# Three-pass gates in eighteen more steps, a plain first product, and an order shifted by a list of moves

## The chip, the cores and the metric

The kernel runs on one core of one Trainium2 chip. The metric is the device time of one execution in microseconds; the number compared is the median of several runs. Beside it stands one profiled execution, whose trace gives the span from the first to the last instruction and the duration of each instruction. The engines are named as in the profile: PE (TensorE, matmuls), PEld (its weight loads, which overlap), DVE (VectorE), ACT (ScalarE), POOL (GpSimd), and SP, whose queue issues nearly all DMAs.

## The reference, cut to what matters

A batch of 32 graphs shares one adjacency matrix of 512 x 512; each node has 128 features. Four layers follow each other, each with a layer norm and a ReLU in front and a residual around it.

```
h = relu(layernorm(x));  x = x + (A_norm @ h) @ W.T + b          # layer 0
h = relu(layernorm(x));  x = x + ggnn(h)                          # layer 1
h = relu(layernorm(x));  x = x + elu(attention(h, adj))           # layer 2
h = relu(layernorm(x));  x = x + attention(h, adj)                # layer 3

def ggnn(h):                       # 5 steps; both matrices are adj
    m  = adj @ h ;  av = [m, m]
    z  = sigmoid(av @ w3.T + h @ u3.T + biases)
    r  = sigmoid(av @ w4.T + h @ u3.T + biases)
    hv = tanh(av @ w5.T + (r * h) @ u5.T + biases)
    h  = (1 - z) * h + z * hv
```

All data are fp32. Since av is m twice, each gate needs one product of m with the sum of two halves of a weight.

## The kernel before, in words

**Tiles.** One batch is one tile of 128 partitions x 512 elements (four chunks of 128 nodes), one PSUM bank wide. PSUM is cut into eight such banks. A batch lives in SBUF through all four layers.

**Stages.** `gcn` is layer 0 for a pair of batches, `ggnn` is layer 1 with five calls of `step`, and `gat` is an attention layer, called twice per batch. For batches 0 to 3 the first layer uses plain products (`product`, L658), from batch 4 on `in_three`. Up to six batches (lanes) are in `ggnn` at a time, while others are in `gcn` and `gat`.

**Products in three passes.** A plain fp32 matmul leaves two records in the trace. `in_three` (L628) replaces it: `operands` (L614) splits the moving tile into upper (ACT, L617), lower (DVE, L618) and across (DVE, L620), and the matrix has been split once into three factors by `factors_of` (L418). Each term is then a matmul in the one-pass format fp32r. Two passes are summed in the bank, ACT rescales the bank in place (`rescale`, L625), and the third pass is added. So a product of adj and h is 12 one-pass matmuls (L644) and one rescaling.

**Gates.** `step` (L750) computes the three gates. `by_m` (L760) multiplies m by a gate weight, either plainly (L755, where m has been copied from PSUM by ACT, L655) or in three passes (L758). For three passes m itself is split by `operands` (L654), each gate's bank is rescaled between its second and third pass, and a fourth rescaling by the inverse stands between the gates r and z, which share a bank (L793). The products of hT by u3 and of r * h by u5 stay plain (L755). `SPLIT_GATES` (L29) says which steps take three passes: all five of batches 2 to 29. Batches 0, 1, 30 and 31 take their gates plainly.

**The order.** Nothing is written in program order. Every operation is given to a planner (`Plan`, L60) with its engine, a cost, a due time, and what it reads and writes. The planner plays the program through as a list schedule (`attempt`, L167): on each engine the ready operation with the smallest `soon` starts, if its buffers are free. `run` (L105) makes eight trials for each of two settings; in the later trials an operation's `soon` is its latest start in a pass backwards (`put_off`, L138), and only operations that started at or before `near_end` (0 us) keep their written due time. The best trial's order is emitted. The loads at the start, the factors and the norms are operations like any other; each engine and SP's queue then run their list in that order.

**The norm.** `norm_relu` (L516) makes mean and variance on DVE, four small operations on POOL (L520 to L525), which the planner takes to cost 1.2 us each, and four scaled ReLUs on ACT (L527).

**The end.** Attention of the last four batches (`near`) avoids round trips through DRAM; the largest piece of DVE work there is L914 (four per attention), PE mixes in L926.

Of the kernel before, what the change touches and what calls it, by code (L numbers as in the profile page):

```python
# [10 lines left out]
F32 = mybir.dt.float32  # L11
# [3 lines left out]
ALU = mybir.AluOpType  # L15

P = 128
EPS = 1e-5
STEPS = 5
# [6 lines left out]
IDLE_FROM = 1342  # L26
RUN_UP = 8
LANES = 6
SPLIT_GATES = {(b, s) for b in range(2, 30) for s in range(STEPS)}  # L29

# [5 lines left out]
SPLIT = 4096.0  # L38
BELOW = 1 - 2.0 ** -13
# [20 lines left out]
class Plan:  # L60
# [44 lines left out]
    def run(self):  # L105


        self.before = {o: [] for o in self.ops}
        for o in reversed(self.ops):
            o.tail = o.cost + o.delay + max((q.tail for q in o.then), default=0)  # L110
            o.first, o.after = o.waits, len(o.then)
            for q in o.then:
                self.before[q].append(o)
        self.uses = {v: v.uses for o in self.ops for v in o.vals}
        best = math.inf, None
        for last, hurry in self.ends:
            for again in range(8):
                if again:
                    late = self.put_off()
                for o in self.ops:  # L120
                    if not again:

                        o.soon = min(o.due, last - o.tail * hurry)
                    else:
                        o.soon = late[o] / self.SLOT if o.at > self.near_end else o.due
                self.attempt()
                if self.end < best[0]:
                    best = self.end, [o.soon for o in self.ops]
                if self.end == math.inf:
                    break  # L130
        assert best[1], "the order has come to a stop"
        for o, soon in zip(self.ops, best[1]):
            o.soon = soon
        self.attempt()
        for o in self.order:
            o.emit()

    def put_off(self):  # L138

# [131 lines left out]
def gnn_stack(ctx: ExitStack, tc: tile.TileContext, a: dict, out: bass.AP):  # L271
    nc = tc.nc
    x, adj = a["x"], a["adj"]
    B, N, D = x.shape
    C = N // P
# [9 lines left out]
    def flat(t):  # L285
# [31 lines left out]
        "rstd": tiles(8, SMALL, "rstd"),  # L317
        "off": tiles(6, SMALL, "off"),
        "rden": tiles(3, SMALL, "rden"),
    }, [(167, 0.1), (181, 0.05)], 0,  # L320
        IDLE_FROM, lambda v: nc.tensor.transpose(v.t[:, 0, :], ident.t, ident.t))
    op = plan.op
    MM, MM1, TURN, MR = 0.858, 0.224, 0.111, 0.2325
# [71 lines left out]
    turned = []  # L395
# [22 lines left out]
    def factors_of(mT, name, due, *then):  # L418


        upper, lower, across = [fixed([P, C, N], name + k, C, dtype=F32R) for k in ("1", "2", "3")]
        for c in range(C):
            op("ACT", COPY, due, lambda c=c: nc.scalar.mul(upper.t[:, c, :], mT.t[:, c, :], BELOW), r=[mT, *then], w=[upper[c]])
            op("DVE", V, due, lambda c=c: nc.vector.tensor_sub(
                lower.t[:, c, :], mT.t[:, c, :], upper.t[:, c, :].bitcast(F32)), r=[mT, upper[c]], w=[lower[c]])
            op("DVE", V, due, lambda c=c: nc.vector.scalar_tensor_tensor(
                across.t[:, c, :], upper.t[:, c, :].bitcast(F32), -1 / SPLIT, lower.t[:, c, :].bitcast(F32),
                op0=ALU.mult, op1=ALU.add), r=[lower[c], upper[c]], w=[across[c]])
            op("ACT", COPY, due, lambda c=c: nc.scalar.mul(
                lower.t[:, c, :], lower.t[:, c, :].bitcast(F32), SPLIT), w=[lower[c]])  # L430
        return upper, lower, across

    def edges(l, c, mask, at, due, *then):
# [38 lines left out]
    def factors_of_gates(due):  # L472
        upper, lower, across = [fixed([P, 3, P], "gates" + k, dtype=F32R) for k in ("1", "2", "3")]
        some = gates.t[:, 1:, :]
        op("ACT", 0.4, due, lambda: nc.scalar.mul(upper.t, some, BELOW), r=[gates], w=[upper])
        op("DVE", 0.47, due, lambda: nc.vector.tensor_sub(lower.t, some, upper.t.bitcast(F32)), r=[gates, upper], w=[lower])
        op("DVE", 0.47, due, lambda: nc.vector.scalar_tensor_tensor(
            across.t, upper.t.bitcast(F32), -1 / SPLIT, lower.t.bitcast(F32), op0=ALU.mult, op1=ALU.add),
           r=[lower, upper], w=[across])
        op("ACT", 0.4, due, lambda: nc.scalar.mul(lower.t, lower.t.bitcast(F32), SPLIT), w=[lower])  # L480
        return upper, lower, across
    of_gates = factors_of_gates(5)
    u5T = transposed(-15.2, (one(raw["u5"]), 0.5), then=turned)
# [32 lines left out]
    def norm_relu(b, y, due, times=None):  # L516

        xb, off, rstd = xs[b], Val("off"), Val("rstd")
        mv = norm_stats(b, due)
        op("POOL", 1.2, due, lambda: nc.gpsimd.tensor_tensor(rstd.t, mv.t[:, :, 1], eps.t, ALU.add), r=[mv, eps], w=[rstd])  # L520
        op("POOL", 1.2, due, lambda: nc.gpsimd.tensor_tensor(rstd.t, rstd.t, mhalf.t, ALU.pow), r=[mhalf], w=[rstd])  # L521
        op("POOL", 1.2, due, lambda: nc.gpsimd.tensor_tensor(off.t, mv.t[:, :, 0], minus1.t, ALU.mult), r=[mv, minus1], w=[off])
        if times:
            op("DVE", 0.1, due, lambda: nc.vector.tensor_mul(rstd.t, rstd.t, times.t), r=[times], w=[rstd])
        op("POOL", 1.2, due, lambda: nc.gpsimd.tensor_tensor(off.t, off.t, rstd.t, ALU.mult), r=[rstd], w=[off])  # L525
        for c in range(C):
            op("ACT", 0.385, due, lambda c=c: nc.scalar.activation(  # L527
                chunk(y, c), xb.t[:, c, :], AF.Relu, bias=off.t[:, c:c + 1], scale=rstd.t[:, c:c + 1]),
               r=[xb[c], off, rstd], w=[y[c * len(y.writers) // C]])
# [27 lines left out]
    def center_relu(b, y, due):  # L557

        xb, st, mv, off, ve, rstd = xs[b], Val("st", C), Val("mv", 2), Val("off", 2), Val("ve"), Val("rstd")
        for a in range(2):  # L560
            both = slice(2 * a, 2 * a + 2)
            for c in (2 * a, 2 * a + 1):
                op("DVE", 0.2, due, lambda c=c: nc.vector.bn_stats(st.t[:, c, :], xb.t[:, c, :]), r=[xb[c]], w=[st[c]])  # L563

            def aggr(a=a, both=both):
                for c in (2 * a, 2 * a + 1):
                    nc.vector.bn_aggr(mv.t[:, c, :], st.t[:, c, :])
                nc.vector.tensor_scalar_mul(off.t[:, both], mv.t[:, both, 0], -1.0)
            op("DVE", 0.22, due, aggr, r=[st[2 * a], st[2 * a + 1]], w=[mv[a], off[a]])
            for c in (2 * a, 2 * a + 1):  # L570
                op("ACT", 0.385, due, lambda c=c: nc.scalar.activation(
                    y.t[:, c, :], xb.t[:, c, :], AF.Relu, bias=off.t[:, c:c + 1]), r=[xb[c], off[a]], w=[y[c]])
        op("DVE", 0.1, due, lambda: nc.vector.tensor_scalar_add(ve.t, mv.t[:, :, 1], EPS), r=[mv], w=[ve])
        op("POOL", 1.0, due, lambda: nc.gpsimd.tensor_tensor(rstd.t, ve.t, mhalf.t, ALU.pow), r=[ve, mhalf], w=[rstd])
        return rstd

    def chunk(h, c):
# [44 lines left out]
           r=[lower, upper], w=[across])  # L622
        return upper, lower, across

    def rescale(p, due, by=1 + 1 / SPLIT):  # L625
        op("ACT", COPY, due, lambda: nc.scalar.mul(flat(p.t), flat(p.t), by), w=[p])  # L626

    def in_three(h, turned, factors, due, split=False):  # L628
# [26 lines left out]
        op("ACT", COPY, due - 6, lambda: nc.scalar.copy(flat(m.t), flat(p.t)), r=[p], w=[m])  # L655
        return m

    def product(h, due):  # L658

        p, m = Val("bank"), Val("m")  # L660
        for c in range(C):
            def times(c=c):
                row = adjT.t[:, c, :]
                terms = [(0, c, row[:, :c * P]), (c, c + 1, diag.t[:, c, :]), (c + 1, C, row[:, (c + 1) * P:])]
                for lo, hi, right in terms:
                    if lo < hi:
                        nc.tensor.matmul(flat(p.t)[:, lo * P:hi * P], h.t[:, c, :], right, start=c == lo == 0,  # L667
                                         stop=c == C - 1, skip_group_check=True)
            op("PE", MM, due, times, r=[h[c], adjT, diag[c]], w=[p, m])
        op("ACT", COPY, due, lambda: nc.scalar.copy(flat(m.t), flat(p.t)), r=[p], w=[m])  # L670
        return m

# [23 lines left out]
    def gcn(pair, due):  # L696
# [8 lines left out]
                xs[b].t, xs[b].t, b0.t[:, None, :].to_broadcast([P, C, D])), r=[b0], w=[xs[b]])  # L705
            ys.append(y)

        ms = [product(y, due + i) if first else in_three(y, False, factors["an"], due + i) for i, y in enumerate(ys)]
        if b == 1:
            factors["adj"] = factors_of(adjT, "adj", -3.6, ys[0])  # L710
            factors["an"] = normalized(ms[0])
# [19 lines left out]
    def ggnn(b, due):  # L731
# [9 lines left out]
        turned = False  # L741
        for s in range(STEPS):
            now = due + LANES * s
            split = (b, s) in SPLIT_GATES
            m = in_three(h, turned, factors["adj"], now, split)
            if b == 4 and s == 0:
                op("SP", 0.0, now, lambda: None, r=[m[0] if split else m], w=[third], delay=0)
            h, turned, hT = step(b, s, m, hT, now, lane)

    def step(b, s, m, hT, due, lane):  # L750
# [39 lines left out]
        op("DVE", V, due - 5, lambda: nc.vector.scalar_tensor_tensor(flat(rh.t), flat(r.t), 1.0, flat(hT.t), op0=ALU.add, op1=ALU.mult),  # L790
           r=[r, hT], w=[rh])
        if split:
            rescale(gate, due - 5, 1 / (1 + 1 / SPLIT))  # L793
        by_m(gate, 2, due + 0.3, False)
        op("ACT", A, due - 5, lambda: nc.scalar.activation(flat(z.t), flat(gate.t), AF.Tanh, bias=gate_b["w3"].t, scale=0.5),  # L795
           r=[gate, gate_b["w3"]], w=[z])
# [238 lines left out]
```

## Time and profile before

| what | value |
|---|---|
| median of three runs | 1515.34 us (1513.87 to 1516.15) |
| the profiled execution's own time | 1513.58 us |
| its span, first to last instruction | 1511.7 us |
| PE busy | 1498.9 us, 99% |
| DVE busy | 1430.9 us, 95% |
| ACT busy | 1236.2 us, 82% |
| POOL busy | 292.9 us, 19% |
| granted TensorE clock | 1.000 |
| share of the DMA engines' time, main queue | 39.6% |

Times are microseconds from the start of the span unless marked ns. A group line names the source line, the engine, the operation, output<-input, the shapes and the count; then the busy time and the mean duration of one in ns; then the idle time of the engine ahead of these instructions and who ended it. In the slices, each digit is the busy share of one fortieth of the span in tenths. A piece of the chain has its start, its length, and the line with the number of instructions in it. DVE and ACT records overlap a little when instructions follow each other closely, so their spacing is shorter than a record.

### The profile page before, as it was taken

Reading aid. Unit: us, or ns where it says so; the run is one execution under the profiler, and the core shown is the slowest. Engines: PE = TensorE matmul, PEld = TensorE weight load, DVE = VectorE, ACT = ScalarE, POOL = GpSimd, SP = SyncE. Lnnn points to the kernel's source line nnn. Section 1 sums busy time; section 2 is a strip of 40 time slices with the busy share of each in tenths; the row PEclk is TensorE's granted clock in tenths of the full one; section 3 lists DMA queues with packets and bytes.
Section 4 is the critical chain, followed back from the end, with each engine's and each line's share of the span. In section 5 each row is a group of like instructions: output and inputs, shape, how many; then the busy total and the mean of one; then the engine's idle time right before and its main releaser. Section 6 shows DMA issues by size and latency. Waiting matters only on the chain.

```text
span 1511.7 us, 24916 instructions
## 1 busy us (share of the span) xinstructions
PE 1498.9 (99%) x7366; PEld 1153.8 (76%) x7366; DVE 1430.9 (95%) x3431; ACT 1236.2 (82%) x2720; POOL 292.9 (19%) x496
## 2 busy tenths in 40 slices
PE   8999999999999999999999999999999999999998
PEld 7666677777777777777787877877777787767788
DVE  8989989999999999999999999999999999898798
ACT  7966888888888888988889888798988978877764
POOL 5412010221221211220222121111221110111111
PEclk9999999999999999999999999999999999999999
DMA  4143333444434444444444453444434444342111
GB/s 112 36 95 108 84 90 106 116 122 119 112 102 116 126 120 127 124 112 105 124 120 101 113 133 105 113 119 120 126 91 127 120 104 118 86 132 71 36 41 44
DMA packets 270151, 157.77 MB, mean 104 GB/s; under 512 B 81248, under 2 KB 236224, under 8 KB 270016
## 3 DMA queue, kind: packets, MB, share of 16 engines
q1 hardware_dynamic: 269728, 155.66, 39.6%
q8 instruction: 58, 0.95, 0.3%
q14 instruction: 77, 0.63, 0.1%
q10 hardware_dynamic: 288, 0.52, 0.1%
HBM read 86.25 MB, written 69.84 MB: 103 GB/s over the span
## 4 chain that ended last, share of the span: by engine, by line
PE 95%; DVE 3%; ACT 1%; DMA 1%; issue 0%; ACTq 0%
PE bank L644 34%; PE bank L755 21%; PE bank L758 19%; PE bank L940 13%; PE bank L871 4%; PE bank L717 2%; PE bank L926 1%; PE bank L586 1%; DVE e L914 1%; DMA rh<-in_L_gnn_w_w_dram 0%; DMA e<-in_adj_dram 0%; PE bank L667 0%; DVE x L721 0%; DVE st L563 0%; DVE e L685 0%
## 5 line engine op out<-in xcount | busy, mean ns | idle before, releaser
L626 ACT ACTIVATE bank<-bank 128x512 f32<-128x512 f32 x748 | 426.6, 595 | 103.3 <-PE bank L644 72.8
L520 POOL TENSOR_TENSOR rstd<-mv,eps 128x4 f32<-128x4 f32 x119 | 59.2, 497 | 1110.2 <-DVE mv L512 1049.1
L940 PEld LDWEIGHTS bank<-h_gat,e 128*128 128x128 f32 x1792 | 218.1, 191 | 24.2 <-issue 17.0
L620 DVE SCALAR_TENSOR_TENSOR across<-lower,upper 128x512 fp32r<-128x512 f32 x328 | 219.7, 676 | 4.2 <-PE bank L758 2.4
L940 PE MATMUL bank<-h_gat,e 128*128 128x129 f32 x1792 | 220.3, 275 | 0.0
L758 PE MATMUL bank<-upper,gates 128*128 128x512 f32 x420 | 205.2, 489 | 0.0
L758 PE MATMUL bank<-across,gates 128*128 128x512 f32 x420 | 198.8, 487 | 0.2 <-ACT bank L626 0.2
L644 PE MATMUL bank<-adj,upper 128*128 128x512 f32 x640 | 189.6, 418 | 0.7 <-ACT upper L617 0.7
L644 PE MATMUL bank<-adj,across 128*128 128x512 f32 x640 | 189.8, 419 | 0.0
L644 PE MATMUL bank<-adj,lower 128*128 128x512 f32 x640 | 175.4, 396 | 0.0
L758 PE MATMUL bank<-lower,gates 128*128 128x512 f32 x420 | 165.5, 394 | 0.0
L755 PE MATMUL bank<-hT,wT 128*128 128x512 f32 x320 | 163.3, 592 | 0.0
L755 PE MATMUL bank<-rh,wT 128*128 128x512 f32 x320 | 163.3, 592 | 0.0
L914 DVE SCALAR_TENSOR_TENSOR e<-row,h_gat,maskT 128x512 f32<-128x512 f32 x224 | 156.8, 741 | 0.0
L644 PEld LDWEIGHTS bank<-adj,across 128*128 128x128 f32 x640 | 118.3, 188 | 42.4 <-issue 16.5
L644 PEld LDWEIGHTS bank<-adj,upper 128*128 128x128 f32 x640 | 118.3, 188 | 41.1 <-issue 14.4
L644 PEld LDWEIGHTS bank<-adj,lower 128*128 128x128 f32 x640 | 120.5, 188 | 28.6 <-DVE lower L618 0.4
L788 ACT ACTIVATE r<-bank,gate_bw 128x512 f32<-128x512 f32 x160 | 111.7, 698 | 36.8 <-PE bank L755 34.6
L521 POOL TENSOR_TENSOR rstd<-rstd,mhalf 128x4 f32<-128x4 f32 x119 | 135.6, 1140 | 0.0
L801 DVE TENSOR_TENSOR hv<-hv,hT 128x512 f32<-128x512 f32 x160 | 108.7, 680 | 19.1 <-ACT hv L799 18.3
L795 ACT ACTIVATE z<-bank,gate_bw 128x512 f32<-128x512 f32 x160 | 110.4, 692 | 18.1 <-PE bank L758 15.4
L799 ACT ACTIVATE hv<-bank,gate_bw 128x512 f32<-128x512 f32 x160 | 111.2, 696 | 11.9 <-PE bank L755 11.7
(162 smaller groups left out, 2843.3 us busy)
## 6 DMA issues: line engine op xcount, KB each, us to landing
far<-sq SPq DMA_DIRECT2D x928, 64.0 KB
h<-far SPq DMA_DIRECT2D x148, 256.0 KB
gT<-far SPq DMA_DIRECT2D x56, 256.0 KB
row<-line SPq DMA_DIRECT2D x56, 256.0 KB
hT<-far SPq DMA_DIRECT2D x112, 64.0 KB
x<-in_x_dram SPq DMA_DIRECT2D x24, 256.0 KB
out_dram<-x SPq DMA_DIRECT2D x20, 256.0 KB
adjT<-in_x_dram SPq DMA_DIRECT2D x8, 256.0 KB
```

The source lines that it names most:

```text
L521: op("POOL", 1.2, due, lambda: nc.gpsimd.tensor_tensor(rstd.t, rstd.t, mhalf.t, ALU.pow), r=[mhalf], w=[rstd])
L620: op("DVE", V, due - 5, lambda: nc.vector.scalar_tensor_tensor(flat(across.t), flat(lower.t).bitcast(F32), -SPLIT, flat(upper.t).bitcast(F ...
L626: op("ACT", COPY, due, lambda: nc.scalar.mul(flat(p.t), flat(p.t), by), w=[p])
L644: nc.tensor.matmul(flat(p.t), left.t[:, c, :], right.t[:, c, :], start=first and c == 0, stop=c == C - 1, skip_group_check=True)
L755: nc.tensor.matmul(flat(p.t), (of or gates).t[:, i, :], flat(moving.t), start=start, stop=True, skip_group_check=True)
L758: nc.tensor.matmul(flat(p.t), of.t[:, i - 1, :], flat(moving.t), start=start, stop=True, skip_group_check=True)
L788: op("ACT", A, due - 5, lambda: nc.scalar.activation(flat(r.t), flat(gate.t), AF.Tanh, bias=gate_b["w4"].t, scale=0.5), r=[gate, gate_b["w ...
L795: op("ACT", A, due - 5, lambda: nc.scalar.activation(flat(z.t), flat(gate.t), AF.Tanh, bias=gate_b["w3"].t, scale=0.5), r=[gate, gate_b["w ...
L799: op("ACT", A, due - 5, lambda: nc.scalar.activation(flat(hv.t), flat(cand.t), AF.Tanh, bias=gate_b["w5"].t), r=[cand, z, gate_b["w5"]], w ...
L801: op("DVE", V, due - 5, lambda: nc.vector.tensor_sub(flat(hv.t), flat(hv.t), flat(hT.t)), r=[hT], w=[hv])
L914: op("DVE", 0.661, due + 3, lambda j=j: nc.vector.scalar_tensor_tensor(e.t[:, j, :], matrix(row), h.t[:, j, D + 1:D + 2], mask.t[:, j, :], ...
L940: nc.tensor.matmul(pt()[:, c, :D + 1], e.t[:, j, i * P:(i + 1) * P], h.t[:, j, :D + 1], start=(j == 0), stop=(j == C - 1))
```

## The change

1. Three-pass gates in all steps but two. `SPLIT_GATES` gives way to `WHOLE_GATES`, the steps that stay plain: the first steps of batches 0 and 1.
2. The first step of batch 0 (`WHOLE`) takes its adjacency product in plain fp32 by `product`, which gets a flag `loops`; with the flag off the rows of adjT are used whole.
3. The scale of the split of the fixed matrices: the upper factor is divided by SPLIT = 4096, the lower factor is made with its scale at once, so its separate scaling on ACT is dropped. The bank is rescaled by SPLIT + 1 instead of 1 + 1 / SPLIT, and by the inverse between r and z.
4. The planner: other POOL costs, `near_end` 12 instead of 0, ten trials instead of eight, and `nudge`. For each number of a list it draws a window of time, a share and a distance from a hash, and shifts `soon` of that share of the operations that started in the window, if they started after `near_end`, by a hashed amount up to that distance, forwards or backwards.

```diff
-SPLIT_GATES = {(b, s) for b in range(2, 30) for s in range(STEPS)}
+WHOLE = {(0, 0)}
+WHOLE_GATES = {(0, 0), (1, 0)}
+
+NUDGES = (
+    582105, 147139, 36044, 562756, 451743, 52419, 574539, 43563, 131, 944493, 237051, 489767, 324034, 993924,
...
+)
...
-            for again in range(8):
+            for again in range(10):
...
-        for o, soon in zip(self.ops, best[1]):
-            o.soon = soon
+        self.nudge(*best)
         self.attempt()
...
+    def nudge(self, end, soon, at):
...
+        for o, t in zip(self.ops, soon):
+            o.soon = t
+        for n in NUDGES:
+            a, b, c, d = (mixed(n * 2654435761 + j * 40503) / 2.0 ** 32 for j in range(1, 5))
+            width = 20 * 40 ** a
+            begin, share, far = b * (end + width) - width, 65536 * 0.01 ** c, 0.02 * 100 ** d
+            for o, t in zip(self.ops, at):
+                if max(self.near_end, begin) < t < begin + width:
+                    m = mixed(n * 2654435761 + o.id * 2246822519 + 77)
+                    if (m & 0xffff) < share:
+                        o.soon += far * ((m >> 16) / 32768 - 1)
...
-    }, [(167, 0.1), (181, 0.05)], 0,
+    }, [(167, 0.1), (181, 0.05)], 12,
...
-            op("ACT", COPY, due, lambda c=c: nc.scalar.mul(upper.t[:, c, :], mT.t[:, c, :], BELOW), r=[mT, *then], w=[upper[c]])
+            op("ACT", COPY, due, lambda c=c: nc.scalar.mul(upper.t[:, c, :], mT.t[:, c, :], BELOW / SPLIT), r=[mT, *then], w=[upper[c]])
+            op("DVE", V, due, lambda c=c: nc.vector.scalar_tensor_tensor(
+                lower.t[:, c, :], upper.t[:, c, :].bitcast(F32), -SPLIT, mT.t[:, c, :], op0=ALU.mult, op1=ALU.add),
+               r=[mT, upper[c]], w=[lower[c]])
             op("DVE", V, due, lambda c=c: nc.vector.tensor_sub(
-                lower.t[:, c, :], mT.t[:, c, :], upper.t[:, c, :].bitcast(F32)), r=[mT, upper[c]], w=[lower[c]])
-            op("DVE", V, due, lambda c=c: nc.vector.scalar_tensor_tensor(
-                across.t[:, c, :], upper.t[:, c, :].bitcast(F32), -1 / SPLIT, lower.t[:, c, :].bitcast(F32),
-                op0=ALU.mult, op1=ALU.add), r=[lower[c], upper[c]], w=[across[c]])
-            op("ACT", COPY, due, lambda c=c: nc.scalar.mul(
-                lower.t[:, c, :], lower.t[:, c, :].bitcast(F32), SPLIT), w=[lower[c]])
+                across.t[:, c, :], lower.t[:, c, :].bitcast(F32), upper.t[:, c, :].bitcast(F32)),
+               r=[lower[c], upper[c]], w=[across[c]])
...
-        op("POOL", 1.2, due, lambda: nc.gpsimd.tensor_tensor(rstd.t, mv.t[:, :, 1], eps.t, ALU.add), r=[mv, eps], w=[rstd])
-        op("POOL", 1.2, due, lambda: nc.gpsimd.tensor_tensor(rstd.t, rstd.t, mhalf.t, ALU.pow), r=[mhalf], w=[rstd])
-        op("POOL", 1.2, due, lambda: nc.gpsimd.tensor_tensor(off.t, mv.t[:, :, 0], minus1.t, ALU.mult), r=[mv, minus1], w=[off])
+        op("POOL", 0.5, due, lambda: nc.gpsimd.tensor_tensor(rstd.t, mv.t[:, :, 1], eps.t, ALU.add), r=[mv, eps], w=[rstd])
+        op("POOL", 1.15, due, lambda: nc.gpsimd.tensor_tensor(rstd.t, rstd.t, mhalf.t, ALU.pow), r=[mhalf], w=[rstd])
+        op("POOL", 0.42, due, lambda: nc.gpsimd.tensor_tensor(off.t, mv.t[:, :, 0], minus1.t, ALU.mult), r=[mv, minus1], w=[off])
...
-    def rescale(p, due, by=1 + 1 / SPLIT):
+    def rescale(p, due, by=SPLIT + 1):
...
-    def product(h, due):
+    def product(h, due, loops):
...
-                terms = [(0, c, row[:, :c * P]), (c, c + 1, diag.t[:, c, :]), (c + 1, C, row[:, (c + 1) * P:])]
+                terms = [(0, C, row)]
+                if loops:
+                    terms = [(0, c, row[:, :c * P]), (c, c + 1, diag.t[:, c, :]), (c + 1, C, row[:, (c + 1) * P:])]
...
-            split = (b, s) in SPLIT_GATES
-            m = in_three(h, turned, factors["adj"], now, split)
+            split = (b, s) not in WHOLE_GATES
+            m = product(h, now, False) if (b, s) in WHOLE else in_three(h, turned, factors["adj"], now, split)
...
-            rescale(gate, due - 5, 1 / (1 + 1 / SPLIT))
+            rescale(gate, due - 5, 1 / (SPLIT + 1))
```

`factors_of_gates` (L472) is changed in the same way as `factors_of`, with one operation of 384 elements in place of four of 512. The list has 175 numbers.

## The prediction, made before the changed kernel was built

> **What bounds the kernel now.** I read the busy table and the forty slices first, then the chain of work that ended last, then a table of busy times by stage, then the groups of instructions by shape, and last the timeline of the tail.
>
> ```profile
> PE 1498.9 (99%) x7366; PEld 1153.8 (76%) x7366; DVE 1430.9 (95%) x3431; ACT 1236.2 (82%) x2720; POOL 292.9 (19%) x496
> ...
> PE   8999999999999999999999999999999999999998
> ...
> DVE  8989989999999999999999999999999999898798
> ACT  7966888888888888988889888798988978877764
> ...
> PE 95%; DVE 3%; ACT 1%; DMA 1%; issue 0%; ACTq 0%
> ```
>
> TensorE (PE) is full in all but the first and last slices, and 95% of the chain lies on it. VectorE (DVE) is close behind. So what leaves PE shortens the kernel, provided that DVE keeps up. The chain also gives PE's true prices, because its pieces run from start to start:
>
> ```profile
> 45.31 2.79 PE bank L644 x12
> ...
> 51.20 2.57 PE bank L755 x6
> ...
> 644.79 2.10 PE bank L758 x9
> ```
>
> Twelve one-pass matmuls of an adjacency product take 2.79 us. Three plain products with 512 columns (each two records) take 2.57 us, 0.857 each. Nine one-pass gate matmuls take 2.10, so a gate product in three passes costs 0.70. By stage (columns: stage, PE, weight loads, DVE, ACT, POOL, clock, DMA):
>
> ```profile
> 60.00:100.00 40.00, 40.00 (x153) 27.41 (x152) 34.73 (x77) 31.97 (x65) 7.48 (x12) 1.00 0.37 82
> 100.00:150.00 50.00, 50.00 (x188) 33.95 (x187) 45.87 (x124) 32.27 (x58) 11.28 (x24) 1.00 0.38 102
> 150.00:200.00 50.00, 50.00 (x190) 34.40 (x189) 45.81 (x89) 43.38 (x87) 4.61 (x8) 1.00 0.33 80
> ...
> 1300.00:1340.00 40.00, 40.00 (x179) 28.73 (x178) 36.85 (x77) 32.60 (x73) 4.18 (x8) 1.00 0.37 103
> 1340.00:1380.00 40.00, 40.00 (x177) 28.27 (x176) 34.38 (x79) 29.40 (x60) 4.89 (x11) 1.00 0.38 104
> 1380.00:1420.00 40.00, 40.00 (x203) 29.85 (x202) 34.68 (x76) 32.77 (x77) 6.54 (x7) 1.00 0.21 55
> 1420.00:1460.00 40.00, 40.00 (x235) 30.88 (x235) 33.48 (x101) 24.83 (x65) 5.78 (x7) 1.00 0.13 40
> 1460.00:1512.00 52.00, 45.94 (x404) 45.03 (x402) 46.91 (x160) 24.11 (x85) 4.06 (x5) 0.98 0.14 42
> ```
>
> The reader should see PE at 40 of 40 up to 1460 us, DVE with some idle time in the same stages, and a tail after 1460 in which neither is full. PE's idle time in the whole span is 1511.7 - 1498.9 = 12.8 us: 5.8 before 60 us, 1.3 in the middle, about 6 in the tail. In the tail PE waits for DVE:
>
> ```profile
> 1496.43 1.16 PE L926 MATMUL bank<-h_gat,e 128*128 128x129 f32 x8 [1.08 <-DVE e L914]
> ...
> 1501.42 6.42 PE L926 MATMUL bank<-h_gat,e 128*128 128x129 f32 x56
> ```
>
> **What the Trainium skill says.** FP8 and Floating Point Precision, TensorE Precision Notes: true fp32 takes four passes through the array, the reduced form reads fp32 and truncates. The trace agrees: 0.857 us against 0.233, 3.7 to one, so three single passes undercut one true fp32 product. VectorE: DVE Perf Modes, the section on the TRN2 errata, prices a vector operation from SBUF at 58 + FD cycles of 0.96 GHz, 594 ns for 512 elements; in this trace full-width DVE operations follow each other at 0.60 us (records of 0.68 overlap). Perfetto Trace Analysis, Optimization Strategy: a kernel can have regimes with different most-contended engines, and the gaps of each regime must be read by themselves. That holds here: PE up to 1460 us, DVE from then on.
>
> **The change, part by part.** Eighteen more steps take the gates in three passes: steps 1 to 4 of batches 0 and 1, and all ten of batches 30 and 31. Their plain m products lie at 37 to 193 us and at 1284 to 1459 us (120 records, twenty steps).
>
> - PE, removed: 18 steps x (2.57 - 2.10) = 8.5 us, 3.8 early and 4.7 late, all on the chain except perhaps the last step or two, which end where the tail begins.
> - PE, added: the first step of batch 0 takes its adjacency product in plain fp32, 4 x 0.857 = 3.43 instead of 2.79, +0.6. It no longer waits for the factors of adj, at a time (before 40 us) when PE has gaps and DVE is full, so this may cost nothing; I count it in full. Net PE: -7.8 us.
> - DVE, added: a split step makes the lower and across operands of m:
>
> ```profile
> L618 DVE TENSOR_TENSOR lower<-bank,upper 128x512 fp32r<-128x512 f32 x140 | 94.7, 676 | 9.7 <-ACT upper L617 9.2
> L626 ACT ACTIVATE bank<-bank 128x512 f32<-128x512 f32 x748 | 426.6, 595 | 103.3 <-PE bank L644 72.8 <-PE bank L758 28.2
> L429 ACT ACTIVATE adj<-adj 128x512 fp32r<-128x512 f32 x4 | 2.5, 632 | 0.7 <-DVE adj L426 0.7
> ```
>
>   18 x 2 x 0.60 = 21.6 us, less 1.2 for batch 0's first step. Early that is 8 x 1.2 = 9.6 us, where DVE has 13.6 us idle between 60 and 200 us (140 - 126.4); PE's saving takes 3.8 of that, so DVE would stand at 99%. Some of its work can slide into the stages after 200 us. Late it is 12 us, where DVE has 20.6 us idle between 1300 and 1460 and loses 4.7 to the shorter PE stage. So the work fits with little to spare in both places. If that cover is gone, each missing microsecond of DVE costs one.
> - ACT, added: four rescalings of a bank and one upper in place of the copy of m, so 4 x 0.595 = 2.4 us a step, 43 us in all, less 5.5 us for nine removed scalings of the factors (four of 632 ns, four of 621, one of 517) and some 1.2 for the first step. ACT is idle 32.4 us of the 140 early (19 needed) and 40.4 of the 160 late (24 needed). It is not the bound, but an ACT instruction now stands between the second and third pass of each gate, and r, z and hv queue behind it on ACT. A step becomes some 3 to 4 us longer; in the middle of the kernel, where 140 such steps already run, PE's waits for such rescalings sum to 14.2 us of weight loads in 48 places and are hidden behind other matmuls. PE costs nothing from this while other lanes have work, but the last step of batch 31 (its m product at 1458 us) feeds the tail directly.
> - For these waits and the full DVE I take +1.0 early (bounds 0 and 3.8, all of the saving) and +1.2 late (bounds 0 and 4.7): the late value is the two new DVE operations of the very last step.
> - The factors keep their number of DVE operations, with subtract and multiply-add exchanged (676 to 686 ns each); the rescaling by 4097 is the same instruction with another constant. Zero.
> - Order: the planner's POOL costs fall from 1.2 to what the trace shows (0.50, 1.14, 0.39, 0.44 us), operations that started before 12 us keep their written order, ten trials replace eight, and the list shifts due times. No instruction is added. The written order issues the gate weights w4 and w3 on SP's queue before the loads of x for batches 1 to 3; before, w4 was issued at 5.55 us and PE waited for it until 10.37. What is moved is the loads of x1 to x3, by a microsecond or two, with their statistics on DVE behind them. PE's first product also waits for the normalised batch 0, so at most 1 us is gained here, and about as much can be lost.
> - What a better order can reach at all: 12.8 us of PE idle, less 1.05 before the first matmul and 3.9 after the last one, leaves 7.9. The bounds are -7.9 and, if a shuffled order leaves new holes on the chip, +3. I take half of the 7.9: -4.0.
>
> Sum: -7.8 + 1.0 + 1.2 - 4.0 = -9.6 us. On the profiled execution: span 1511.7 - 9.6 = 1502.1, its own time 1513.58 - 9.6 = 1504.0. The median of the three runs shown is 1.76 above that execution: 1515.34 - 9.6 = 1505.7.
>
> **The rivals.**
> - Nearly all reachable holes close and DVE hides everything: -7.8 - 7.9 = -15.7, so 1499.6. For it: a long list of moves can serve many holes. Against: the tail is DVE work that waits for the last batches, and more DVE work is added.
> - The tail swallows the late part: DVE ends when it ended before, so the 4.7 late are lost and the order gives nothing. Then -3.8 + 0.6 + 1.0 = -2.2, so 1513.1. For it: from 1432 us on DVE has hardly a hole of more than half a microsecond. Against: the 20.6 us of idle time just ahead.
> - Slower: DVE becomes the bound of the late stage. Its holes before 1460 us are waits for results of the last lanes (2.3 us for hv at 1426), and if only u of the needed 12 us falls into them, the end moves by 12 - u, with the early part still at -2.2: faster than before only while u is over 9.8, and out of measurement's reach on the slow side below u = 6.8. With u = 4 it gives -2.2 + 8 = +5.8, so 1521.1. Against it: the middle of the kernel runs with DVE at 99.5% (500 to 700 us, 199.0 of 200) and PE full.
> - The list moves nothing that matters (order 0): -5.6, so 1509.7; it belongs to the forecast's own range.
>
> **How the numbers follow.** A measurement of this kernel can tell about 0.2%, 3.0 us, from no change: 1512.3 to 1518.4 is "same". Forecast 0.58 (own range 1501.5 to 1511), all holes closed 0.14, tail swallows 0.17, slower 0.11. Of the third, a third falls below 1512.3, the rest within; of the fourth, 0.03 stays within. Faster 0.58 + 0.14 + 0.06 = 0.78, same 0.11 + 0.03 = 0.14, slower 0.08. The range 1498 to 1515 leaves out about 0.05 below and 0.12 above.
>
> **What would show it.** In the profile after: plain gate products of m in 12 records instead of 120; gate groups of 474 in place of 420; rescalings 819 in place of 748; PE busy some 8 us less (1491); DVE busy 1451; no scaling of lower in the factors. PE still full from some 40 us to beyond 1440 would show that DVE hid the new work; PE idle in the first 200 us or from 1300 on with DVE as releaser would show that it did not. PE idle of about 9 us in all would confirm the order's term. The prediction is wrong if DVE's idle time before 1460 us stays as large as it was while the tail begins later, or if PE's price for a three-pass gate at the two ends is above 0.70.

## The result, and the profile after

| what | before | after |
|---|---|---|
| median of five runs | 1515.34 us (1513.65 to 1516.15) | 1510.13 us (1508.32 to 1513.26) |
| ratio | | 0.9969, 95% interval 0.9955 to 0.9982 |
| profiled execution: own time, span | 1513.58, 1511.7 us | 1510.13, 1508.2 us |

The change is faster by 0.31%, 4.7 us with an interval of 2.7 to 6.8; forecast were 9.6. (The ratio is made from all runs of both kernels; the two medians alone are 5.2 us apart.) Measured again on another occasion it gave 1510.37 us, ratio 0.9974 (0.9964 to 0.9983). Its runs lie 5 us apart, those of before 2.5.

The page of the profile after: the busy table, the slices of PE, DVE and ACT, and the chain that ended last.

```profile
PE 1494.0 (99%) x7416; PEld 1160.5 (77%) x7416; DVE 1446.5 (96%) x3465; ACT 1258.1 (83%) x2781; POOL 294.6 (20%) x496
...
PE   9999999999999999999999999999999999999998
...
DVE  8999989999999999999999999999989999998999
ACT  6788888888988898878888888888878798978874
...
DVE 5%; PE 1%; issue 0%; ACT 0%; POOL 0%; DVEq 0%
```

The counts are as the prediction had them (PE 7366 - 54 x 2 + 162 - 12 + 8 = 7416). But PE is busy only 4.9 us less, and its idle time, 1508.2 - 1494.0 = 14.2 us, has grown from 12.8 although the span is shorter. The chain is no help here: its shares add up to some 6% because it could be followed back only through the tail. The stages say where PE stands still (columns as in the prediction's table):

```profile
40.00:60.00 20.00, 17.28 (x72) 12.54 (x71) 16.69 (x53) 14.60 (x31) 8.38 (x17) 1.00 0.14 27
...
100.00:150.00 50.00, 50.00 (x198) 35.88 (x197) 49.83 (x126) 41.22 (x78) 12.39 (x22) 1.00 0.40 103
...
500.00:700.00 200.00, 198.80 (x995) 155.78 (x994) 195.05 (x456) 168.02 (x372) 40.00 (x66) 1.00 0.44 115
700.00:900.00 200.00, 198.49 (x972) 153.25 (x971) 194.00 (x447) 168.59 (x375) 39.47 (x67) 1.00 0.44 114
...
1420.00:1460.00 40.00, 39.78 (x252) 33.19 (x251) 39.11 (x105) 33.44 (x89) 6.13 (x8) 1.00 0.17 47
1460.00:1512.00 52.00, 44.28 (x381) 42.71 (x379) 45.23 (x164) 24.38 (x82) 5.47 (x5) 0.97 0.14 41
```

The kernel before, in two of these stages:

```profile
500.00:700.00 200.00, 200.00 (x998) 156.26 (x997) 199.01 (x459) 172.92 (x389) 36.82 (x64) 1.00 0.46 121
700.00:900.00 200.00, 200.00 (x988) 156.44 (x987) 194.79 (x474) 169.75 (x371) 44.82 (x76) 1.00 0.45 116
```

Between 100 and 150 us DVE is full (49.8 of 50) and PE loses nothing; from 1300 to 1460 us PE loses 0.5 us in all. So the added work at the two ends is nearly hidden. The holes are elsewhere: one of 2.7 us in 40 to 60 us, and new ones in the middle of the kernel, where no step was changed. Before, PE was full from 60 to 1100 us. From 60 to 1300 us PE's idle time grew from 1.3 to 4.4 us. The waits name the new waiter: ScalarE's ReLUs of the norm, which wait for the last GpSimd operation of that norm (total, times, longest). Before:

```profile
ACT y L527 <- POOL off L525: 0.4, 1, 0.4
```

After, 24.6 us in all:

```profile
ACT y L565 <- POOL off L563: 19.2, 15, 3.8
ACT h L565 <- POOL off L563: 5.4, 3, 3.4
```

The timeline around one such hole shows the whole way (start, length, engine, line; in brackets the idle time and who ended it):

```profile
604.84 0.67 DVE L841 TENSOR_TENSOR hv<-hv,hT 128x512 f32<-128x512 f32 x1
605.42 0.69 DVE L658 SCALAR_TENSOR_TENSOR across<-lower,upper 128x512 fp32r<-128x512 f32 x1
605.48 3.10 POOL L558 TENSOR_TENSOR rstd<-mv,eps 128x4 f32<-128x4 f32 x1
...
607.83 0.69 DVE L658 SCALAR_TENSOR_TENSOR across<-lower,upper 128x512 fp32r<-128x512 f32 x1
608.43 0.71 DVE L632 STREAM_TRANSPOSE sq<-hT 128x512 f32<-128x512 f32 x1
608.53 0.20 POOL L563 TENSOR_TENSOR off<-off,rstd 128x4 f32<-128x4 f32 x1
...
608.76 1.65 ACT L565 ACTIVATE y<-x,off,rstd 128x128 f32<-128x128 f32 x4 [3.80 <-POOL off L563]
...
610.32 0.57 ACT L664 ACTIVATE bank<-bank 128x512 f32<-128x512 f32 x1
...
610.94 1.20 PE L682 MATMUL bank<-adj,across 128*128 128x512 f32 x4 [1.01 <-ACT bank L664]
```

A GpSimd addition of 4 elements per partition, which takes 0.2 us when it is short, takes 3.10. It ends with the run of VectorE operations with two SBUF tensors (604.84 to 608.52), as the first VectorE operation with one input, a transpose, begins. The addition belongs to the next norm, but it stands in GpSimd's queue ahead of the multiplication (608.53) that the ReLUs need. ScalarE has put four ReLUs next in its queue and waits 3.80 us; behind them stands the rescaling of a bank; PE needs that bank and stops. The holes at 44 us (2.7), 847 us (1.5) and 1114 us (1.4) begin in the same way, behind GpSimd operations of 5.1, 3.0 and 2.1 us. What stands behind the ReLUs differs: at 44 us a copy of m for PE, at 847 us a rescaling, at 1114 us an operand that VectorE needs before PE.

### The profile page after: what moved, and what is told of

Read it like the earlier page. It is cut to its first block, busy times and chain, and to the rows that moved or that the text cites. A ratio compares the mean times of both kernels' runs of the same rounds, so it can differ in the third digit from the quotient of the medians.

```text
span 1508.2 us, 25120 instructions
## 1 busy us (share of the span) xinstructions
PE 1494.0 (99%) x7416; PEld 1160.5 (77%) x7416; DVE 1446.5 (96%) x3465; ACT 1258.1 (83%) x2781; POOL 294.6 (20%) x496
## 5 line engine op out<-in xcount | busy, mean ns | idle before, releaser
L664 ACT ACTIVATE bank<-bank 128x512 f32<-128x512 f32 x819 | 464.9, 595 | 85.2 <-PE bank L682 59.2
L798 PE MATMUL bank<-upper,gates 128*128 128x512 f32 x474 | 232.9, 491 | 0.4 <-ACT bank L664 0.2
L658 DVE SCALAR_TENSOR_TENSOR across<-lower,upper 128x512 fp32r<-128x512 f32 x345 | 230.6, 677 | 2.7 <-PE bank L798 0.9
L558 POOL TENSOR_TENSOR rstd<-mv,eps 128x4 f32<-128x4 f32 x119 | 54.3, 456 | 894.9 <-DVE mv L550 842.7
L798 PE MATMUL bank<-across,gates 128*128 128x512 f32 x474 | 217.7, 473 | 0.0
L798 PE MATMUL bank<-lower,gates 128*128 128x512 f32 x474 | 186.7, 394 | 0.0
L559 POOL TENSOR_TENSOR rstd<-rstd,mhalf 128x4 f32<-128x4 f32 x119 | 143.5, 1206 | 1.3
L565 ACT ACTIVATE y<-x,off,rstd 128x128 f32<-128x128 f32 x252 | 113.0, 497 | 15.4 <-POOL off L563 15.1
L798 PEld LDWEIGHTS bank<-across,gates 128*128 128x128 f32 x474 | 88.8, 188 | 45.2 <-ACT bank L664 19.9
```

The lines of the kernel that those rows point to most:

```text
L558: op("POOL", 0.5, due, lambda: nc.gpsimd.tensor_tensor(rstd.t, mv.t[:, :, 1], eps.t, ALU.add), r=[mv, eps], w=[rstd])
L559: op("POOL", 1.15, due, lambda: nc.gpsimd.tensor_tensor(rstd.t, rstd.t, mhalf.t, ALU.pow), r=[mhalf], w=[rstd])
L565: op("ACT", 0.385, due, lambda c=c: nc.scalar.activation(chunk(y, c), xb.t[:, c, :], AF.Relu, bias=off.t[:, c:c + 1], scale=rstd.t[:, c:c ...
L798: nc.tensor.matmul(flat(p.t), of.t[:, i - 1, :], flat(moving.t), start=start, stop=True, skip_group_check=True)
```

## Theories and experiments

**Theory A.** GpSimd's small operations are locked out while VectorE runs operations with two SBUF inputs. The order now leaves them no slack, because the plan takes them at their mean duration, and ScalarE's queue carries the delay to PE. **Theory B.** An order pressed by a list of moves is fragile by itself; any jitter opens holes. **Theory C.** The added VectorE work of the eighteen steps fills VectorE, and that costs what is missing.

All times are medians, with the ratio to the kernel before in runs of the same occasion and its 95% interval.

### GpSimd's part left out, in the order of after and of before

```diff
-        op("POOL", 0.5, due, lambda: nc.gpsimd.tensor_tensor(rstd.t, mv.t[:, :, 1], eps.t, ALU.add), r=[mv, eps], w=[rstd])
+        small(0.5, due, lambda: nc.gpsimd.tensor_tensor(rstd.t, mv.t[:, :, 1], eps.t, ALU.add), r=[mv, eps], w=[rstd])
...
+    def small(cost, due, emit, r, w):
+        def sometimes():
+            if o.at < 80:
+                emit()
+        op("POOL", cost, due, sometimes, r=r, w=w)
+        o = plan.ops[-1]
```

> The changed kernel in its own order, but the four small GpSimd operations of each norm are left out once the plan is past 80 us; the ReLUs then read an older norm's scale and offset. In the changed kernel PE has holes of 1.0, 1.5 and 1.4 us at 611, 847 and 1114 us, each behind a ReLU on ScalarE that waited 2.3 to 3.8 us for a stretched GpSimd operation. Theory A (GpSimd operations stretch while VectorE is busy, the order leaves them no slack, and ScalarE's queue carries the delay to PE): those holes go, span 1500 to 1503, time about 1503, and the spread of the runs shrinks. Theory B (the order made by the list is fragile by itself, any jitter opens holes): the holes stay in number and size, time 1508 to 1511. Theory C (the added VectorE work fills VectorE): holes stay where VectorE is full, time 1507 to 1510.

1503.78 us, ratio 0.9929 (0.9917 to 0.9942), runs 3.0 us apart. The page:

```profile
PE 1491.4 (99%) x7416; PEld 1160.1 (77%) x7416; DVE 1445.9 (96%) x3465; ACT 1258.3 (84%) x2781; POOL 47.2 (3%) x76
```

The stages in the middle:

```profile
500.00:700.00 200.00, 200.00 (x1006) 157.33 (x1004) 196.87 (x460) 169.68 (x373) 0.00 (x0) 1.00 0.45 117
700.00:900.00 200.00, 200.00 (x980) 154.52 (x979) 195.72 (x462) 171.11 (x380) 0.00 (x0) 1.00 0.46 115
```

The holes at 610, 847 and 1114 us are gone. The same matmuls in the same order keep PE 2.6 us less busy (probably short waits that hide under the ends of the records before them) and idle for 10.2 us instead of 14.2. The hole at 44 us, before the 80 us from which operations are left out, is still there. VectorE did not become faster for lack of GpSimd: it is busy 1445.9 us against 1446.5.

> The control: the kernel before in its own order with the same GpSimd operations left out past 80 us. Its plan took each of them at 1.2 us, more than twice the mean of three of the four. Theory A: they already had slack, so the time stays within 1513.5 to 1516. If leaving them out saves as much here as in the changed kernel (5 us or more), it is not the slack that differs and theory A falls.

1514.1 us, ratio 1.0000 (0.9992 to 1.0009). Before, these operations cost nothing that can be measured (the interval leaves 1.3 us); after, they cost (0.9969 - 0.9929) x 1514.4 = 6.1 us, with an uncertainty of some 3 us. So the delay is GpSimd's, as theory A has it; B, in the form that any jitter does it, falls, since DMAs and all other engines still ran in the same pressed order. The pair doesn't show why the order of after has no room for the delay. The kernel before has six GpSimd operations of over 2 us too, four of them past 80 us (up to 3.56), but its ReLUs wait only 0.4 us for GpSimd.

### The disputed cost by itself

> The disputed cost by itself; nothing of the reference is computed. Pairs of the small GpSimd operations (128 x 4, an add and a power) run six times: alone, beside back-to-back scalar_tensor_tensor of two SBUF tensors, beside tensor_sub of two SBUF tensors, beside tensor_add of a PSUM and an SBUF tensor, beside stream transposes, beside bn_stats. Theory A: alone the add takes 0.19 us and the power 1.0; beside back-to-back operations of two SBUF tensors single GpSimd operations take 1.5 to 5 us, beside the one-input operations they stay near their time alone. If they stretch in no phase, or in all alike, the stretching in the kernel has another cause.

Five lines of its timeline: scalar_tensor_tensor in the first two, tensor_sub in the next three.

```profile
15.13 28.99 DVE L33 SCALAR_TENSOR_TENSOR w<-x,y 128x512 f32<-128x512 f32 x48
...
16.44 1.46 POOL L54 TENSOR_TENSOR q<-s,half 128x4 f32<-128x4 f32 x1
...
44.11 28.98 DVE L36 TENSOR_TENSOR w<-x,y 128x512 f32<-128x512 f32 x48
44.28 28.87 POOL L49 TENSOR_TENSOR s<-s,gate 128x4 f32<-128x4 f32 x1 [6.12 <-DVE gate L48]
73.10 0.20 POOL L53 TENSOR_TENSOR q<-s,half 128x4 f32<-128x4 f32 x1
```

Beside 48 subtractions of two SBUF tensors one GpSimd addition took 28.87 us: it got in only after the last of them. Beside scalar_tensor_tensor of two SBUF tensors the addition took 0.42 to 0.65 and the power 1.46, against 0.20 and 1.01 alone. Beside an addition that takes one input from PSUM, beside transposes and beside bn_stats both took their time alone. My expectation was half wrong: the fused operation (scalar_tensor_tensor) stretches GpSimd's but does not lock it out here. In the kernel it does keep GpSimd out: four of the six operations of the lock above are of this form, and the steps alone, below, show five of them in a row. Why the two differ stays open. The Trainium skill has the lock (SBUF — State Buffer, section Who interferes with whom: a VectorE instruction with two SBUF inputs contends with a GpSimd instruction that reads SBUF, through a shared port pair that is held as an exclusive lock). This trace agrees for the subtractions and shows only a stretching for scalar_tensor_tensor; it adds that GpSimd didn't get in between any two of the 48 subtractions.

### What the list and the planner's costs do

```diff
-NUDGES = (582105, 147139, ...
+NUDGES = ()
```

> The changed kernel with an empty list: the steps, the plain first product, the new planner costs and trials stay. Theory A: the low GpSimd costs are still in the plan, so ScalarE's waits for GpSimd stay at 15 us or more in total and the time is 1505 to 1511, no better than the changed kernel by more than 3 us. Theory B: without the list the waits for GpSimd fall to a few us and the time is 1502 to 1505, better than the changed kernel. If the list works on the chip as meant, it is slower than the changed kernel: 1513 or more.

1506.80 us, ratio 0.9947 (0.9934 to 0.9959). Without the list the changed kernel is faster by 0.22% (3.3 us in the medians). The intervals overlap a little with the first measurement of the changed kernel (0.9955 to 0.9982), not with the second (0.9964 to 0.9983). ScalarE waits 15.0 us for GpSimd instead of 24.6, in pieces of at most 2.6 us that PE seldom feels. Neither theory fits in full: A allowed at most 3 us of gain, B expected the waits to fall to a few us.

> The changed kernel with an empty list and the old GpSimd costs of 1.2 us in the plan (1.0 for the near norm). Theory A: ScalarE's waits for GpSimd fall to under 3 us, PE's holes between 300 and 1300 us to under 2 us, time 1504 to 1508, faster than the run without the list and with low costs, although that one's order looks shorter to the planner. Theory B: no difference between the two beyond 1.5 us. Theory C: holes in the first 200 us and from 1300 us on with VectorE as releaser, time 1509 or more.

1506.51 us, ratio 0.9948 (0.9935 to 0.9962); the waits for GpSimd fall to 1.1 us. The time does not: theory A's claim that this alone would make it faster than the run above was wrong, and no difference is what theory B expected here. So the low costs by themselves have no measured price. That they hurt together with a list, which uses up the slack they promise, is a reading and not shown: the list of the change was not run with costs of 1.2 us.

### The steps alone

Planner as before: costs of 1.2 us, eight trials, near_end 0, no list.

> The eighteen three-pass steps, the plain first product and the new scale of the factors, with the planner as it was before: GpSimd costs 1.2 us, eight trials, near_end 0, no list. The sum of the prediction without its order term is -7.8 + 1.0 + 1.2 = -5.6 us. Theory A (the steps pay as counted, the order took it back): 1505.5 to 1509.5, faster than the whole change. Theory C (the added VectorE work took it back): 1510 to 1514.

1512.69 us, ratio 0.9986 (0.9980 to 0.9993): 2.1 us gained, within what theory C expected. A hole lies at the late end, where steps were added, but behind GpSimd again:

```profile
1377.71 4.53 POOL L548 TENSOR_TENSOR off<-off,rstd 128x4 f32<-128x4 f32 x1
...
1378.48 0.69 DVE L826 TENSOR_TENSOR hv<-hv,hT 128x512 f32<-128x512 f32 x1
...
1379.08 0.69 DVE L643 SCALAR_TENSOR_TENSOR across<-lower,upper 128x512 fp32r<-128x512 f32 x1
...
1381.49 0.69 DVE L996 SCALAR_TENSOR_TENSOR v<-v,adjT 128x512 f32<-128x512 f32 x1
...
1382.27 1.26 ACT L550 ACTIVATE y<-x,off,rstd 128x128 f32<-128x128 f32 x3 [2.17 <-POOL off L548]
...
1384.07 0.50 PE L783 MATMUL bank<-across,gates 128*128 128x512 f32 x1 [1.91 <-ACT bank L649]
```

A lock of 4.53 us exceeds what the plan had set aside even at 1.2 us per operation. After the last subtraction (1378.48) five scalar_tensor_tensor follow each other up to 1382.18, and GpSimd gets in only then.

> The run with the steps alone (planner as before, no list) took 1512.7 us, 3 to 7 us more than the sum of the prediction without its order term. Here its order is kept and the GpSimd operations of the norms are left out past 80 us (the ReLUs read an older norm's values). Theory A: its hole of some 5 us between 1380 and 1420 us, with GpSimd operations of 4.5 and 4.9 us in it, goes, and the time is 1505.5 to 1508.5, PE's own saving of 7.8 us in full. Theory C (the added VectorE work is what the steps cost): 1511 or more.

1507.94 us, ratio 0.9960 (0.9947 to 0.9972). 0.9986 - 0.9960 = 0.0026, 3.9 us (some 2 either way), were GpSimd's; the steps gain 6.1 us without it. What is left for theory C is 1.7 us (7.8 - 6.1), no more than the uncertainty. VectorE is not out of it, though: GpSimd waited for an uninterrupted run of VectorE's operations, and from 1340 to 1380 us VectorE is busy 39.9 of 40 us, where it was 34.4 before. That the added work makes these runs longer is likely, but not shown. So an order without any list can fall into the lock too, and at costs of 1.2 us. The whole change with costs of 1.2 us and no list differs from the steps alone only in near_end 12 and ten trials, and is 1512.69 - 1506.51 = 6.2 us faster. Its trace has seven GpSimd operations of over 2 us against five here, but its ReLUs wait 1.1 us for GpSimd against 4.1: up to 3.9 of the gain can be that nobody waits behind its locks.

> As the run with the steps alone, but the first step of batch 0 keeps its adjacency product in three passes. By PE's prices it should be 0.6 us faster than with the plain product: 1505 to 1509. If the plain product's worth is that it need not wait for the factors while VectorE is full in the first 40 us, it is slower by 1 us or more: 1509 to 1512, with the added idle time of PE before 60 us.

1511.95 us, ratio 0.9979 (0.9972 to 0.9987), 0.7 us less than with the plain product in the medians, the sign and size that PE's prices give, but the intervals overlap. Its PE is busy 54.72 us before 60 us, against 56.27 with the plain product, of which 0.6 is less work: some idle time is won by the plain product there and is lost again later. Its worth is not settled.

### A list that knows the delay

> The changed kernel with GpSimd costs of 1.2 us in the plan and another list of 38 moves, found by keeping each random move that shortens the planner's own order under these costs. Theory A: with slack for most GpSimd operations a list pays on the chip: ScalarE's waits for GpSimd stay under 8 us, time 1500 to 1505, below the 1506.5 of the same kernel with an empty list. Theory B (a list makes the order fragile whatever the costs): 1507 to 1511.

1501.77 us, ratio 0.9916 (0.9903 to 0.9930). This is another list, found under the costs of 1.2 us; its ReLUs wait 1.7 us for GpSimd. A list as such is not fragile: theory B falls in its second form, that any list makes the order so.

The next plan keeps GpSimd out while VectorE has two SBUF inputs:

```diff
-            if busy[e]:
+            if busy[e] or e == "POOL" and locked():
                 return
...
+            elif kind == 0 and o.engine == "POOL":
+                held.append(o)
...
+            if held and not locked():
+                o = held.pop()
+                busy["POOL"] = False
+                post(now + o.delay, 1, o)
+                start("POOL")
```

> No list, but the planner knows what the run of GpSimd beside VectorE showed: a GpSimd operation neither starts nor ends while VectorE is in an operation with two SBUF inputs, and costs 0.25 us (1.2 for a power) otherwise. No instruction is added or left out. Theory A: ScalarE's waits for GpSimd fall to under 4 us and no hole of PE over 1 us has a GpSimd operation behind it: 1504 to 1507. If the lock is not what delays the GpSimd operations, such holes stay and the time is 1508 or more.

1506.05 us, ratio 0.9948 (0.9934 to 0.9961). ScalarE's ReLUs have no wait for GpSimd left in the list of waits. Without a list it is no faster than the plan with 1.2 us: 0.9948 both.

> The planner with the lock of GpSimd beside VectorE, and a third list of 38 moves found by keeping each random move that shortens the order under that plan. Theory A (a list pays as far as the plan knows what delays GpSimd): 1498 to 1502.5, ScalarE's waits for GpSimd under 4 us, no hole of PE over 1 us between 100 and 1400 us. Theory B (a list makes an order fragile whatever the plan): 1504 or more.

1499.88 us, ratio 0.9907 (0.9892 to 0.9922), with a list of 39 moves (not 38). It beats the kernel before by 14.1 us and the changed one by 10.1 (0.9974 - 0.9907, of 1514.2). Against the other list under costs of 1.2 us (0.9903 to 0.9930) the intervals overlap. Its page and its one wait of a ReLU for GpSimd (total, times, longest):

```profile
PE 1491.1 (100%) x7418; PEld 1162.3 (78%) x7418; DVE 1448.3 (97%) x3465; ACT 1262.7 (84%) x2781; POOL 284.4 (19%) x496
```

```profile
ACT y L565 <- POOL off L563: 1.0, 1, 1.0
```

PE does the work of the changed kernel and is idle for 1497.6 - 1491.1 = 6.5 us instead of 14.2.

> The changed kernel once more, on the same chip as the run beside it, as the yardstick for the versions: 1508 to 1513. Theory A: the holes that come from GpSimd operations of over 2 us fall at the same places as in the first profile (611, 847, 1114 us, within a few us), since the order of VectorE's operations is the same in each execution. If jitter made them, they fall elsewhere.

1510.37 us, ratio 0.9974 (0.9964 to 0.9983). The holes at 43 (2.73 us), 610 (1.01) and 1112 us (1.44) are back in the second profile with GpSimd operations of 5.11, 3.09 and 2.11 us, equal to the first within 0.01 us; the one at 847 us is not. Of the six GpSimd operations of over 2 us in the first profile, four come back. So most locks belong to the order of VectorE's queue, and some depend on how two queues happen to meet, which fits the wide spread of the runs.

## Why the prediction was wrong, point by point

- **PE's work** was right in count and price. In the changed kernel without GpSimd's part, whose chain can be followed, nine one-pass gate matmuls at the late end take 2.10 us (at 1309.68) and four at the early end 0.94, and PE is busy 1491.4 us, where 1491 was forecast. The steps without GpSimd's delays gain 6.1 us (4.2 to 8.0), which is the 7.8 counted less 1.7 of waits; I had put 2.2 for these waits, and the two can't be told apart.
- **VectorE's new work** was nearly hidden at both ends as argued, at 49.8 of 50 us between 100 and 150. The 34 added operations were counted right; busy time rose by 15.6 us and not by 20.4, ScalarE's by 21.9 and not by some 36, and where the rest went stays open. The slower rival was wrong. So was the one in which the tail swallows the late part. Its -2.2 us is what the steps alone measured (-2.1), but by coincidence: with GpSimd left out the same order gains 6.1, and PE's idle time after 1460 us fell from 5.8 to 3.9 us in the whole change.
- **The order**: I took -4.0. With GpSimd's part left out in both, the whole change against the steps alone gives (0.9929 - 0.9960) x 1514.4 = -4.7, with an uncertainty of some 3 us. The size fits, but -4.0 was half of a bound and no more than a guess. With GpSimd at work the order gives (0.9969 - 0.9986) x 1514.4 = -2.6.
- **The step that failed** is what the prediction did with GpSimd. It took the small operations at "what the trace shows (0.50, 1.14, 0.39, 0.44 us)" and put no wait behind them into the sum: not into the +2.2 for the waits of the steps, and not into the order, where +3 for new holes stayed a bound. Those are means. The profile before already had single operations of 3.56 and 3.67 us in two of those groups (the first and the third, with means of 0.50 and 0.39). There the ReLUs waited only 0.4 us for GpSimd, and leaving it out past 80 us changed nothing (ratio 1.0000). In the steps alone such delays cost 3.9 us, even with the old costs of 1.2 us in the plan, and in the changed kernel 6.1 us. So the fall of the planner's costs is not the whole of it; how much of the 6.1 it makes stays open.
- In the prediction's terms, the steps were put at -5.6 and measured -2.1, and the order was put at -4.0 and measured -2.6. With GpSimd as a term of its own the sum is -7.8 + 1.7 - 4.7 + 6.1 = -4.7. That it meets the measured ratio is no check, since the terms are differences along one chain of runs, each uncertain by some 2 to 3 us.
- The rival in which the list moves nothing gave 1509.7 us, close to the 1510.13 measured. That is luck: the steps brought less than it says, and the order more.
- I had listed the operations' durations, but not asked who waits behind the ReLU in ScalarE's queue. In two of the four holes it is a bank's rescaling, and so PE.
- At the start PE's idle time before 40 us fell from 5.4 to 2.7 us. The loads' written order and the plain first product can both have a part in it; they were not separated. The hole at 44 us, behind GpSimd, took most of it back: before 60 us it was 5.8 and is 5.5.

## What to carry to other kernels

A plan that gives an operation its mean duration has no place for its longest ones, and an order that is made shorter under such a plan can run into them. Before a padded cost is corrected, look at the longest durations of the operation and at what stands behind its reader in that reader's queue. A long duration need not cost anything by itself: the kernel before had four of over 2 us past 80 us and lost nothing that could be measured. Here both ways to tell the plan of the delay helped: a list found under padded costs took the changed kernel from 1506.5 to 1501.8 us, and one found under a plan that knows the lock from 1506.1 to 1499.9, where the list of the change took it from 1506.8 to 1510.1. The three lists differ, and the first two results are too close to say which way is better.

## What the runs showed of the hardware that I had not expected

- One GpSimd addition waited 28.87 us behind 48 back-to-back subtractions of two SBUF tensors on VectorE; it was not let in between two of them. In the traces of the kernel three to seven GpSimd operations of an execution take 2 to 5 us.
- The form matters in the run by itself: scalar_tensor_tensor of the same two tensors only stretched the addition (0.20 to 0.42, at most 0.65 us) and lengthened the power by 0.45 us, and an operand in PSUM left GpSimd undisturbed (0.20 and 1.01). In the kernel this does not hold: five scalar_tensor_tensor in a row after a subtraction kept a multiplication of 128x4 out for 3 us more. What decides stays open.
